# A lattice, a small conv net and three conv layers: Wu on four column tiles, the lattice's squares on ScalarE

## The chip, the cores and the metric

The kernel runs on one core of one Trainium2 chip. The core has five engines with a queue each: TensorE (PE, the matrix unit; its weight loads are shown as PEld), VectorE (DVE), ScalarE (ACT), GpSimd (POOL) and SyncE (SP). The last two are used here for memory fills and to issue copies (DMAs), which 16 DMA engines carry out. The metric is device time in microseconds (us), lower is better; three runs of the kernel before took 17346.95 us in the median.

## What is computed

The input is 32 images of 8 channels, 256x256, in float32. Four layers, each `x + f(groupnorm(x))`:

```python
# layer 0, on x = _gn(x)
drive = grid = x[:, :8]
for _ in range(15):
    mapped = R * grid * (1.0 - grid)
    local = _conv(mapped, K_local, groups=8)            # 3x3, per channel
    grid = (1.0 - BETA) * ((1.0 - EPS) * mapped + EPS * local) + BETA * drive
cml_out = jnp.clip(grid, 0.0001, 1.0 - 0.0001)
h = jax.nn.relu(_conv(x, Wp, bp))                       # 8 -> 128 channels, 3x3
nca_out = jax.nn.sigmoid(_conv(h, Wu, bu))              # 128 -> 8, 1x1
gin = jnp.concatenate([x, cml_out, nca_out], axis=1)
g = jax.nn.sigmoid(_conv(jax.nn.relu(_conv(gin, Wg1, bg1)), Wg2, bg2))
return g * cml_out + (1.0 - g) * nca_out
# layer 1: a 3x3 conv on x and weights rounded to 8-bit integers (one scale for the whole tensor)
# layer 2: a 3x3 conv in float32;  layer 3: a 5x5 mean filter per channel
```

The scale of layer 1 needs the maximum over all 32 images, so layer 0 runs over all images first, and the layers 1 to 3 follow in a second stage.

## The kernel before

**First stage.** Two strands are woven together by hand in one instruction order. `lattice(b, ahead)` runs the 15 steps of image b. `gated()` runs the net and the gate of image b-1, and is consumed piece by piece: each piece yields an estimate of its TensorE time in us, each point of the lattice yields a gap (`BLOCK`, 7.4, after a half-step), and the loop under `tc.manual_schedule()` takes pieces until the gap is filled. Image 0's lattice has no net beside it, and the last image's net no lattice. `errands(b)`, one item after each half-step, writes the normalised image to DRAM (xn_d with a border, nr_d row by row), loads the next image and takes its statistics.

**The lattice.** Channels 0 to 5 lie as patches of 16x8 pixels over the 128 partitions, 512 columns a channel, in `states[0]` and `states[1]`, three channels each. The kernel keeps v(v-1) of the state, and the constants of the map are folded into the weights. A half-step of three channels is: six matmul calls into three PSUM tiles psc (L368 with the patch, L370 with the ring of neighbours), a sum with the drive on VectorE (L378: `max` with a floor, which only catches NaNs, and an add, from PSUM to the state), the product v(v-1) in place (L384), and `spread(half)`, four copies on SyncE's queue that bring the neighbours of each patch to `rings[half]` (L246). TensorE needs these rings in the same half of the next step. `ps_c`, the pool of psc, has three buffers, and the statistics' small matmuls (L104, L111, L304) take theirs from it too.

Channels 6 and 7 are computed by VectorE alone, in blocks of four rows in `strip`: nine `tap`s a step (L317), three after half 0 and six after half 1, then a floor (L395), the product (L396), and `edges()`, two copies on SyncE's queue (L250, L251) that bring the neighbouring rows.

**The net.** For two blocks of 16 rows (one n, eight to an image) `gated` runs 16 calls ph (L606, one for each row number within the block), a relu on ScalarE into hh (L611), and the 1x1 conv Wu (L582): row r's eight outputs go to 32 PSUM partitions, tile q = r // 4, and within these to the eight that the padded weights `wu_sb[:, i, :]` pick, i = r % 4. Rows are taken four at a time, in the order 0, 4, 1, 5 and then 2, 6, 3, 7 (plus 8 in the second half), and the four Wu calls of a batch come in the next batch, in `second()`. `psum` has three buffers for ph and hh has six. The gate (L508 to L541) reads xq (nr_d), cq (cr_d), the sigmoid nh and the rows beside them, and xc, the image itself. It runs in pieces, one a batch: three conv pieces, the rest, Wg2, VectorE's blend, the store of x1, and at an image's end its statistics.

**Second stage.** Rounds over b: `layer3(b-3)`, `layer2(b-1)`, `layer1(b)`; here the framework's scheduler puts the instructions in order. `layer2` stores its result in x3_d in one copy and loads it again as y, in 16 copies, with a row of the image on each partition, as layer 3 wants it.

An fp32 matmul call is two MATMUL instructions in the profile.

Of the kernel before, what the change touches and what calls it, by code (L numbers as in the profile page):

```python
# [9 lines left out]
F32 = mybir.dt.float32  # L10
BF16 = mybir.dt.bfloat16
AF = mybir.ActivationFunctionType
ALU = mybir.AluOpType
# [34 lines left out]
RQ = 4  # L48
BLOCK = 7.4
STEPS = 15  # L50
# [16 lines left out]
def kernel(  # L67
    ctx, tc, x, patch, ring, taps, pick, wp, bp, wu, bu, wg1, wga, wgb, bg1, wg2, bg2, w1, b1, w2, b2, w3,
    w3h, eye, gavg, gavr, gsel, out,
# [22 lines left out]
    x1_d = [dram.tile([P, NPX], F32, name=f"x1_d{b}") for b in range(B)]  # L92
    x3_d = [dram.tile([P, NPX], F32, name=f"x3_d{b}") for b in range(2)]

# [73 lines left out]
    with ExitStack() as es:  # L168
# [9 lines left out]
        ring_sb = const(wt, ring, [RING, CP, P], "ring_sb")  # L178
        taps_sb = const(wt, taps, [P, 9], "taps_sb")
        pick_sb = const(wt, pick, [P, P], "pick_sb")  # L180
        wp_sb = const(wt, wp, [72, P], "wp_sb")
# [11 lines left out]


        for t in (patch_sb, ring_sb):
            flat = t.rearrange("p c m -> p (c m)")
            nc.vector.tensor_scalar(flat, flat, -R_ * (1.0 - BETA_) * EPS_, None, ALU.mult)
        nc.vector.tensor_scalar(taps_sb, taps_sb, -R_ * (1.0 - BETA_) * EPS_, None, ALU.mult)
        nc.vector.tensor_scalar(
            taps_sb[:, 4:5], taps_sb[:, 4:5], -R_ * (1.0 - BETA_) * (1.0 - EPS_), None, ALU.add  # L200
        )
        for c in range(CP):
            nc.vector.scalar_tensor_tensor(
                patch_sb[:, c, :], eye_sb, -R_ * (1.0 - BETA_) * (1.0 - EPS_), patch_sb[:, c, :],
                ALU.mult, ALU.add,
            )
# [11 lines left out]
        strip = wt.tile([P, RQ + 2, WP], F32, name="strip")  # L218
        for t in (*xbs, nh, zero, *hbs, *states, *rings, strip):
            nc.gpsimd.memset(t, 0.0)  # L220

        xn_d = [dram.tile([C, HP, WP], F32, name=f"xn_d{i}") for i in range(3)]
        nr_d = [dram.tile([P, HB, WP], F32, name=f"nr_d{i}") for i in range(3)]
        cr_d = [dram.tile([P, HB, WP], F32, name=f"cr_d{i}") for i in range(3)]
        for t in xn_d:
# [25 lines left out]
        def errands(b):  # L253
# [27 lines left out]
            if b >= 0:  # L281
                for r in four:
                    nc.gpsimd.dma_start(
                        window(
                            nr_d[b % 3], r.start * C * HB * WP,
                            [[WP, P], [C * HB * WP, 4], [1, WP]],
                        ),
                        xbs[b % 2][:, r, :],
                    )
                    yield  # L290
# [3 lines left out]
            for r in range(0, RB, 2):  # L294
                nc.vector.bn_stats(bn[:, r, :], xb[:, r, 1 : 1 + W])
                nc.vector.bn_stats(bn[:, r + 1, :], xb[:, r + 1, 1 : 1 + W])
                yield
            st, st2 = sts[(b + 1) % 2]
# [8 lines left out]
        def lattice(b, ahead):  # L307
# [42 lines left out]
            for c in range(CP):  # L350
                nc.vector.scalar_tensor_tensor(
                    inner(c), dr[:, c], 1.0, dr[:, c], ALU.subtract, ALU.mult
                )
                nc.scalar.mul(dr[:, c], dr[:, c], BETA_)
                if c == 0:
                    nc.scalar.mul(d2, d2, BETA_)
                if c % HALF == HALF - 1:
                    spread(c // HALF)
                yield 1.5
            yield 4  # L360
            for step in range(STEPS):
                for half in range(2):
# [14 lines left out]
                    for c in mine:  # L377
                        nc.vector.scalar_tensor_tensor(  # L378
                            inner(c), pss[c % HALF], FLOOR, dr[:, c], ALU.max, ALU.add
                        )  # L380
                    for c in mine:
                        v = inner(c)
                        if step < STEPS - 1:
                            nc.vector.scalar_tensor_tensor(v, v, 1.0, v, ALU.subtract, ALU.mult)  # L384
# [30 lines left out]
            for r in range(0, RB, 4):  # L415
                nc.gpsimd.dma_start(
                    window(
                        cr_d[b % 3], r * C * HB * WP,
                        [[WP, HB * CP], [C * HB * WP, 4], [1, WP]],
                    ),  # L420
                    xb[0 : HB * CP, r : r + 4, :],
                )

            row = HB * WP
            for q in range(HB // RQ):
                for c in range(2):
                    at = (C * RQ * q + CP + c) * row
                    nc.sync.dma_start(
                        window(cr_d[b % 3], at, [[WP, HB], [C * row, RQ], [1, WP]]),
                        window(  # L430
                            strip, (2 * q + c) * (RQ + 2) * WP + WP,
                            [[8 * (RQ + 2) * WP, HB], [WP, RQ], [1, WP]],
                        ),
                    )

        def beside_blocks(t, src, q, k0, n, slots):
# [3 lines left out]
            for i, (p, k) in enumerate(((P - C, k0 - 1), (0, k0 + 1))):  # L440
# [8 lines left out]
                for j, m, at in runs:  # L449
# [5 lines left out]
                    )  # L455

        place = [0]

        def gated():
# [22 lines left out]
            def gate(n, quarter):  # L482
# [95 lines left out]
            def second():  # L578
                n, pn, four = late.pop()
                for hh, r in four:  # L580
                    q, i = divmod(r, 4)
                    nc.tensor.matmul(  # L582
                        pn[32 * q : 32 * q + 32, :], wu_sb[:, i, :], hh,
                        start=i == 0, stop=i == 3,
                    )
# [8 lines left out]
            for n in range(B * NCH):  # L594
# [31 lines left out]
            second()  # L626
            yield 1.9
            while due:
# [23 lines left out]
    with ExitStack() as es:  # L652
# [80 lines left out]
        def layer2(b, x2, st):  # L733
# [60 lines left out]
        twos, threes = {}, {}  # L794
        for b in range(B + 3):
            if b >= 3:
                layer3(b - 3, *threes.pop(b - 3))
            if 1 <= b <= B:
                threes[b - 1] = layer2(b - 1, *twos.pop(b - 1))
            if b < B:  # L800
                twos[b] = layer1(b)


def laid_out(inputs):
# [33 lines left out]
    def on_rows(w):  # L838
# [42 lines left out]
    for g in range(4):  # L881
# [5 lines left out]
        ring=ring,  # L887
        taps=np.tile(K[CP:, 0].reshape(2, 9), (P // 2, 1)),
        pick=np.repeat((np.arange(P) == HB * CP)[:, None], P, 1).astype(f),
        wp=inputs["L0_conv_Wp"].transpose(2, 1, 3, 0).reshape(72, P),  # L890
# [44 lines left out]
```

## Time and profile before

| | |
|---|---|
| median of 3 runs | 17346.95 us (17322.46 to 17360.35) |
| time of the profiled execution | 17311.55 us |
| span of the profiled execution | 17309.7 us |
| TensorE clock granted, mean | 0.964 |
| shares of the chain that ended last | PE 73%, DVE 18%, DMA 5%, issue 2% |
| HBM read, written | 1078.72 MB, 404.28 MB |
| DMA moved in all | 2208.48 MB, 128 GB/s |
| first and last start of L325 (an image's lattice begins) | 34.6 us, 14016.5 us |

The span is from the first to the last instruction; 1.85 us of the execution lie around it. A line of a group gives the line of the code, engine, operation, output and inputs with their shapes, the number of instructions, then busy time in us and the mean of one in ns, then the idle time of the engine before them and who ended it. Busy time counts overlapping instructions once, so a group whose count times mean exceeds its busy time had several at work together. An engine that waits is put down to the instruction that released it.

### The profile page before, as it was taken

How to read it: one execution, taken by the hardware profiler on the slowest of the kernel's cores; microseconds unless marked ns; L12 is line 12 of the kernel's file. 1: busy time of each engine (PE TensorE's matmuls, PEld its weight loads, DVE VectorE, ACT ScalarE, POOL GpSimd, SP SyncE). 2: the span in 40 equal slices, each digit the busy share in tenths (PEclk: the TensorE clock that was granted, in tenths of full speed). 3: DMA queues.
4: the chain of work that ended last, by engine and by line, in shares of the span. 5: the costliest groups of instructions: out<-in, count | busy, mean ns of one | idle time of the engine just before them, and what ended most of it. 6: DMA issues, size and time to landing. Idle time of an engine off the chain costs nothing.

```text
span 17309.7 us, 133874 instructions
## 1 busy us (share of the span) xinstructions
PE 16500.7 (95%) x42888; PEld 6670.3 (39%) x42888; DVE 13265.9 (77%) x17529; ACT 4089.7 (24%) x5982; POOL 3931.6 (23%) x6517
## 2 busy tenths in 40 slices
PE   5999999999999999999999999999999999899999
PEld 2333333333333333333333333333333333344444
DVE  8788888888888788878888887888888884555554
ACT  0222222222222222222222222222222223111110
POOL 1222222222222222222222222222222223111111
PEclk7999999999999999999999999999999999999999
DMA  3666666666666666666666666666666665455454
GB/s 82 129 129 133 133 131 134 127 132 132 133 132 131 124 133 134 128 128 128 127 134 130 129 132 129 133 133 132 133 130 131 133 127 117 113 129 125 122 131 102
DMA packets 817532, 2208.48 MB, mean 128 GB/s; under 512 B 281741, under 2 KB 485749, under 8 KB 732741
## 3 DMA queue, kind: packets, MB, share of 16 engines
q0 software_dynamic: 464384, 1425.54, 39.8%
q1 hardware_dynamic: 352452, 774.38, 21.6%
q8 instruction: 350, 5.73, 0.2%
q14 instruction: 346, 2.83, 0.1%
HBM read 1078.72 MB, written 404.28 MB: 86 GB/s over the span
## 4 chain that ended last, share of the span: by engine, by line
PE 73%; DVE 18%; DMA 5%; issue 2%; POOL 1%; SPq 1%; ACT 0%; DVEq 0%; POOLq 0%; ACTq 0%
PE ph L606 15%; PE psc L370 12%; PE psc L368 11%; DVE acc L317 10%; PE pg L508 10%; PE pn L582 8%; PE psv L777 6%; PE psv L698 5%; DMA rings<-state 3%; DVE state L384 2%; DVE state L378 2%; PE psv L702 2%; PE psv L781 1%; PE pq L519 1%; DMA im<-xn_d 1%
## 5 line engine op out<-in xcount | busy, mean ns | idle before, releaser
L317 DVE SCALAR_TENSOR_TENSOR acc<-strip,taps_sb,acc 128x1024 f32<-128x1024 f32 x3840 | 4931.3, 1284 | 120.2
L611 ACT ACTIVATE hh<-ph,bp_sb 128x512 f32<-128x512 f32 x4096 | 2812.2, 687 | 8403.9 <-PE ph L606 8338.9
L606 PE MATMUL ph<-im,wp_sb 72*128 72x512 f32 x8192 | 4042.1, 610 | 108.7 <-DMA im<-xn_d 86.6
L378 DVE SCALAR_TENSOR_TENSOR state<-psc,flat 128x512 f32<-128x512 f32 x2880 | 1894.8, 686 | 2072.5 <-PE psc L370 2009.5
L368 PE MATMUL psc<-state,patch_sb 128*128 128x512 f32 x5760 | 2762.9, 614 | 365.9 <-DVE u L112 284.4
L370 PE MATMUL psc<-rings,ring_sb 80*128 80x512 f32 x5760 | 2796.6, 623 | 81.5 <-DMA rings<-state 81.4
L476 POOL DMA_DIRECT2D im<-xn_d x3072 | 1730.5, 568 | 3501.1 <-PE ph L606 3117.7
L606 PEld LDWEIGHTS ph<-im,wp_sb 72*128 72x128 f32 x8192 | 1486.5, 191 | 2223.6 <-issue 2074.8
L582 PE MATMUL pn<-hh,wu_sb 128*32 128x512 f32 x8192 | 2022.0, 616 | 0.0
L368 PEld LDWEIGHTS psc<-state,patch_sb 128*128 128x128 f32 x5760 | 1073.6, 193 | 1921.4 <-issue 1142.3
L370 PEld LDWEIGHTS psc<-rings,ring_sb 80*128 80x128 f32 x5760 | 1138.5, 199 | 1588.6 <-issue 1550.9
L384 DVE SCALAR_TENSOR_TENSOR state<-state 128x512 f32<-128x512 f32 x2688 | 1689.7, 685 | 0.0
L777 PE MATMUL psv<-xr,w_sb 128*128 128x512 f32 x2560 | 1159.7, 595 | 0.5 <-DVE xr L762 0.5
L541 POOL DMA_DIRECT2D x_d<-xc x256 | 152.0, 594 | 4082.8 <-DVE xc L536 4017.9
L582 PEld LDWEIGHTS pn<-hh,wu_sb 128*32 128x32 f32 x8192 | 394.0, 111 | 1469.9 <-issue 1469.9
L508 PE MATMUL pg<-xq,wg_sb 128*128 128x512 f32 x1536 | 734.7, 615 | 13.0 <-DMA xq<-nr_d 13.0
L508 PE MATMUL pg<-cq,wg_sb 128*128 128x512 f32 x1536 | 735.0, 616 | 0.0
L508 PE MATMUL pg<-nh,wg_sb 128*128 128x512 f32 x1536 | 732.8, 614 | 0.0
L698 PE MATMUL psv<-xh,w_sb 128*128 128x512 f32 x1536 | 704.8, 595 | 8.1 <-DVE xh L734 4.1
L452 POOL DMA_DIRECT2D hb<-nh x576 | 320.4, 560 | 1710.4 <-ACT nh L560 1662.8
L777 PEld LDWEIGHTS psv<-xr,w_sb 128*128 128x128 f32 x2560 | 475.7, 189 | 565.9 <-issue 561.5
L786 DVE TENSOR_TENSOR y<-psv,y 128x512 f32<-128x512 f32 x256 | 176.6, 690 | 623.3 <-PE psv L781 623.0
(155 smaller groups left out, 12270.6 us busy)
## 6 DMA issues: line engine op xcount, KB each, us to landing
im<-xn_d POOLq DMA_DIRECT2D x3072, 193.3 KB, 7.3
rings<-state SPq DMA_DIRECT2D x1920, 159.5 KB
rings<-state SPq DMA_DIRECT2D x1920, 106.3 KB
strip<-strip SPq DMA_DIRECT2D x960, 126.0 KB
xn_d<-xb POOLq DMA_DIRECT2D x128, 516.0 KB, 10.3
nr_d<-xb POOLq DMA_DIRECT2D x128, 516.0 KB, 9.0
xq<-nr_d POOLq DMA_DIRECT2D x128, 516.0 KB, 11.6
cq<-cr_d POOLq DMA_DIRECT2D x128, 516.0 KB, 13.7
```

The costliest lines, as they stand in the source:

```text
L317: nc.vector.scalar_tensor_tensor(acc, strip[:, dy : dy + RQ, dx : dx + W], taps_sb[:, 3 * dy + dx : 3 * dy + dx + 1], d2 if dy == 1 and dx ...
L368: nc.tensor.matmul(pss[-1], patch_sb[:, c, :], inner(c), start=True, stop=False)
L370: nc.tensor.matmul(pss[c % HALF], ring_sb[:, c, :], rings[half][:, c % HALF, 0 : TX * SY].rearrange("p (x y) -> p x y", y=SY)[:, :, 0:TY], ...
L378: nc.vector.scalar_tensor_tensor(inner(c), pss[c % HALF], FLOOR, dr[:, c], ALU.max, ALU.add)
L384: nc.vector.scalar_tensor_tensor(v, v, 1.0, v, ALU.subtract, ALU.mult)
L476: nc.gpsimd.dma_start(im[24 * dy : 24 * dy + 24, k, 0:run], window(xn_d[b % 3], at, [[HP * WP, C], [1, 3], [1, run]]),)
L508: nc.tensor.matmul(o, wg1_sb[:, s, dx, :], src[:, :, dx : dx + W], start=s == dx == 0, stop=False,)
L582: nc.tensor.matmul(pn[32 * q : 32 * q + 32, :], wu_sb[:, i, :], hh, start=i == 0, stop=i == 3,)
L606: nc.tensor.matmul(ph.rearrange("p (k w) -> p k w", w=W), wp_sb, im[:, :, j * WP : j * WP + W], start=True, stop=True,)
L611: nc.scalar.activation(hh, ph, AF.Relu, bias=bp_sb)
L698: nc.tensor.matmul(o, w[:, dx, :], src[:, 2 * i : 2 * i + 2, dx : dx + W], start=dx == 0, stop=False,)
L777: nc.tensor.matmul(o, w3_sb[:, dx, :], xr[:, k, 2 * g : 2 * g + 2, dx : dx + W], start=dx == 0, stop=False,)
```

## The change

- *Wu.* Rows are taken in the order 0 to 3, then 4 to 7; q and i change places, so that the four calls of a batch go to the four tiles of 32 PSUM partitions. The rows of a block thereby lie on the partitions in another order (`turn`, row r at place r % 4 * 4 + r // 4), and everything that is read or written with a row a partition group follows: the weights in `on_rows`, the writes of nr_d and cr_d, and the store of x3.
- *x for the gate.* `errands` writes the raw rows of the next image to a new DRAM tensor xr_d in this order, in four copies; `gate` loads xc from it in one copy instead of two from x.
- *Squares.* VectorE's sum is written back to PSUM, and ScalarE squares it into the state: (v - 0.5)^2 = v(v-1) + 0.25. States and rings are therefore filled with 0.25, and the constant is taken out again by `lift`, a number for each channel that is added to the drive. The first squares of an image are ScalarE's too.
- *Order.* The squares, `spread(half)` and, after half 1, `edges()` are emitted 1.7 us of the net's pieces after VectorE's part. In between `held` is not empty and the gate's statistics don't advance. BLOCK is 6.5, of which 1.7 come first; a Wu group yields 1.05 instead of 1.9.
- *Second stage.* `load1`, the load of x1, is called first in its round; x3 has the image's own layout and is stored in 16 copies, and y is loaded in two.

```diff
-BLOCK = 7.4
+BLOCK = 6.5
...
+        lift = wt.tile([P, CP], F32, name="lift")
+        nc.vector.tensor_reduce(lift, kern_sb, AX.X, ALU.add)
+        nc.vector.tensor_scalar(
+            lift, lift, 0.25 * R_ * (1.0 - BETA_) * EPS_, 0.25 * R_ * (1.0 - BETA_) * (1.0 - EPS_),
+            ALU.mult, ALU.add,
+        )
+        minus = wt.tile([P, 1], F32, name="minus")
+        nc.vector.memset(minus, -0.5)
...
-        for t in (*xbs, nh, zero, *hbs, *states, *rings, strip):
+        for t in (*xbs, nh, zero, *hbs, strip):
             nc.gpsimd.memset(t, 0.0)
+        for t in (*states, *rings):
+            nc.gpsimd.memset(t, 0.25)
...
+                if r < 8:
+                    nc.gpsimd.dma_start(
+                        window(
+                            xr_d[(b + 1) % 3], r // 2 * C * HB * W,
+                            [[W, P], [4 * C * HB * W, 4], [1, W]],
+                        ),
+                        xb[:, 2 * r : 2 * r + 4, 1 : 1 + W],
+                    )
...
-                nc.vector.scalar_tensor_tensor(
-                    inner(c), dr[:, c], 1.0, dr[:, c], ALU.subtract, ALU.mult
-                )
-                nc.scalar.mul(dr[:, c], dr[:, c], BETA_)
+                nc.scalar.activation(inner(c), dr[:, c], AF.Square, bias=minus)
+                nc.scalar.activation(
+                    dr[:, c], dr[:, c], AF.Identity, bias=lift[:, c : c + 1], scale=BETA_
+                )
...
                     for c in mine:
-                        nc.vector.scalar_tensor_tensor(
-                            inner(c), pss[c % HALF], FLOOR, dr[:, c], ALU.max, ALU.add
-                        )
-                    for c in mine:
-                        v = inner(c)
-                        if step < STEPS - 1:
-                            nc.vector.scalar_tensor_tensor(v, v, 1.0, v, ALU.subtract, ALU.mult)
-                        else:
+                        ps = pss[c % HALF]
+                        nc.vector.scalar_tensor_tensor(ps, ps, FLOOR, dr[:, c], ALU.max, ALU.add)
+                    if step == STEPS - 1:
+                        for c in mine:
                             nc.vector.tensor_scalar(
-                                dr[:, c], v, 0.0001, 1.0 - 0.0001, ALU.max, ALU.min
+                                dr[:, c], pss[c % HALF], 0.0001, 1.0 - 0.0001, ALU.max, ALU.min
                             )
-                    if step < STEPS - 1:
-                        spread(half)
...
-                        edges()
...
+                    held.append(half)
+                    yield 1.7
+                    if step < STEPS - 1:
+                        for c in mine:
+                            nc.scalar.activation(inner(c), pss[c % HALF], AF.Square, bias=minus)
+                        spread(half)
+                        if half == 1:
+                            edges()
+                    held.clear()
                     next(ahead, None)
-                    yield BLOCK
+                    yield BLOCK - 1.7
...
-                for k in range(2):
-                    nc.gpsimd.dma_start(
-                        xc[:, k, :],
-                        window(
-                            x, b * C * H * W + (k0 + k) * RB * W, [[W, RB], [H * W, C], [1, W]]
-                        ),
-                    )
+                nc.gpsimd.dma_start(xc, xr_d[b % 3][:, k0 : k0 + 2, :])
...
-                for _ in stats_parts(ps_c, bn, st, gavr_sb, "psc"):
+                parts = stats_parts(ps_c, bn, st, gavr_sb, "psc")
+                more = True
+                while more:
+                    if not held:
+                        more = next(parts, parts) is None
                     yield 0
...
-                    q, i = divmod(r, 4)
+                    i, q = divmod(r, 4)
...
-                    for rows in ((0, 4, 1, 5), (2, 6, 3, 7)):
+                    for rows in ((0, 1, 2, 3), (4, 5, 6, 7)):
...
                                 second()
-                                yield 1.9
+                                yield 1.05
...
-        def layer1(b):
+        def load1(b):
             x1 = two.tile([P, NPX], F32, name="x1")
             nc.gpsimd.dma_start(x1, x1_d[b])
+            return x1
+
+        def layer1(b, x1):
...
-            nc.gpsimd.dma_start(x3, x2)
+            for r in range(RB):
+                m = r % 4 * 4 + r // 4
+                nc.gpsimd.dma_start(
+                    window(x3, r * W, [[H * W, C], [RB * W, HB], [1, W]]),
+                    x2[C * m : C * m + C, :].rearrange("p (k w) -> p k w", w=W),
+                )
...
-            for k in range(HB):
+            for k in range(2):
                 nc.gpsimd.dma_start(
-                    y[RB * (k % 8) : RB * (k % 8) + RB, k // 8, :, :],
-                    window(x3, k * W, [[C * NPX, RB], [NPX, C], [1, W]]),
+                    y[:, k, :, :], window(x3, k * P * W, [[W, P], [H * W, C], [1, W]])
                 )
...
         for b in range(B + 3):
+            if b < B:
+                x1 = load1(b)
...
-        return a.reshape(RB * i, 3, RB * o)
+        turn = np.arange(RB) % 4 * 4 + np.arange(RB) // 4
+        return a[turn][:, :, :, turn].reshape(RB * i, 3, RB * o)
```

More of the change, by code (lines that the diff above doesn't have):

```diff
@@ L67 @@
 def kernel(
-    ctx, tc, x, patch, ring, taps, pick, wp, bp, wu, bu, wg1, wga, wgb, bg1, wg2, bg2, w1, b1, w2, b2, w3,
+    ctx, tc, x, patch, ring, taps, kern, pick, wp, bp, wu, bu, wg1, wga, wgb, bg1, wg2, bg2, w1, b1, w2, b2, w3,
     w3h, eye, gavg, gavr, gsel, out,
@@ L92 @@
     x1_d = [dram.tile([P, NPX], F32, name=f"x1_d{b}") for b in range(B)]
-    x3_d = [dram.tile([P, NPX], F32, name=f"x3_d{b}") for b in range(2)]
+    x3_d = [dram.tile([C, H, W], F32, name=f"x3_d{b}") for b in range(2)]
     def stats_parts(pool, bn, dst, avg, tag):
@@ L179 @@
         taps_sb = const(wt, taps, [P, 9], "taps_sb")
+        kern_sb = const(wt, kern, [P, CP, 9], "kern_sb")
         pick_sb = const(wt, pick, [P, P], "pick_sb")
@@ L218 @@
         strip = wt.tile([P, RQ + 2, WP], F32, name="strip")
-        for t in (*xbs, nh, zero, *hbs, *states, *rings, strip):
+        for t in (*xbs, nh, zero, *hbs, strip):
             nc.gpsimd.memset(t, 0.0)
+        for t in (*states, *rings):
+            nc.gpsimd.memset(t, 0.25)
         xn_d = [dram.tile([C, HP, WP], F32, name=f"xn_d{i}") for i in range(3)]
+        xr_d = [dram.tile([P, HB, W], F32, name=f"xr_d{i}") for i in range(3)]
         nr_d = [dram.tile([P, HB, WP], F32, name=f"nr_d{i}") for i in range(3)]
@@ L284, in errands @@
                         window(
-                            nr_d[b % 3], r.start * C * HB * WP,
-                            [[WP, P], [C * HB * WP, 4], [1, WP]],
+                            nr_d[b % 3], r.start // 4 * C * HB * WP,
+                            [[WP, P], [4 * C * HB * WP, 4], [1, WP]],
                         ),
@@ L417, in lattice @@
                     window(
-                        cr_d[b % 3], r * C * HB * WP,
-                        [[WP, HB * CP], [C * HB * WP, 4], [1, WP]],
+                        cr_d[b % 3], r // 4 * C * HB * WP,
+                        [[WP, HB * CP], [4 * C * HB * WP, 4], [1, WP]],
                     ),
@@ L426, in lattice @@
                 for c in range(2):
-                    at = (C * RQ * q + CP + c) * row
+                    at = (C * q + CP + c) * row
                     nc.sync.dma_start(
-                        window(cr_d[b % 3], at, [[WP, HB], [C * row, RQ], [1, WP]]),
+                        window(cr_d[b % 3], at, [[WP, HB], [4 * C * row, RQ], [1, WP]]),
                         window(
@@ L455, in beside_blocks @@
                     )
+        held = []
         place = [0]
@@ L626, in gated @@
             second()
-            yield 1.9
+            yield 1.05
             while due:
@@ L800 @@
             if b < B:
-                twos[b] = layer1(b)
+                twos[b] = layer1(b, x1)
 def laid_out(inputs):
@@ L888, in laid_out @@
         taps=np.tile(K[CP:, 0].reshape(2, 9), (P // 2, 1)),
+        kern=np.tile(K[:CP, 0].reshape(1, CP, 9), (P, 1, 1)),
         pick=np.repeat((np.arange(P) == HB * CP)[:, None], P, 1).astype(f),
```

## The prediction

> **What bounds the kernel now.** I read the page's busy times first, then its slices.
>
> ```profile
> PE 16500.7 (95%) x42888; PEld 6670.3 (39%) x42888; DVE 13265.9 (77%) x17529; ACT 4089.7 (24%) x5982; POOL 3931.6 (23%) x6517
> ...
> PE   5999999999999999999999999999999999899999
> ...
> DVE  8788888888888788878888887888888884555554
> ...
> PEclk7999999999999999999999999999999999999999
> ```
>
> TensorE is full in every slice but the first, where VectorE is. Is a full TensorE really the limit in each stage? Busy time by stretches answers that: inside the first image, in one steady image of layer 0, and in layers 1 to 3.
>
> ```profile
> core 0: us, PE busy (x) PEld busy (x) DVE busy (x) ACT busy (x) POOL busy (x), PEclk, DMA share, GB/s
> ...
> 200.00:300.00 100.00, 63.93 (x118) 24.94 (x116) 98.25 (x121) 0.00 (x0) 0.00 (x0) 0.80 0.33 62
> ...
> 7000.00:7450.00 450.00, 432.89 (x1131) 172.04 (x1130) 366.42 (x458) 117.99 (x173) 108.69 (x181) 0.97 0.64 130
> ...
> 16000.00:16500.00 500.00, 499.87 (x1305) 222.47 (x1304) 271.87 (x536) 60.19 (x86) 71.42 (x112) 1.00 0.53 129
> ```
>
> So image 0 is VectorE's (98 of 100 us), the next 31 lattices are TensorE's with VectorE at 81%, and everything after about 14450 us is TensorE's alone. The waits of TensorE between 450 and 14400 us show how little else it loses:
>
> ```profile
> PE psc L368 <- DVE u L112: 275.1, 60, 5.0
> PE ph L606 <- DMA im<-xn_d: 56.5, 27, 3.1
> PE psc L370 <- DMA rings<-state: 48.8, 50, 2.8
> ```
>
> These are microseconds in total, times, and the longest. Over 31 images they are 9, 2 and 1.6 us an image. An image takes 452.8 us there, from the ends of the first psc blocks of successive images (image 0 to 1: 408.8 us). Next the groups that the change touches:
>
> ```profile
> L317 DVE SCALAR_TENSOR_TENSOR acc<-strip,taps_sb,acc 128x1024 f32<-128x1024 f32 x3840 | 4931.3, 1284 | 120.2
> L611 ACT ACTIVATE hh<-ph,bp_sb 128x512 f32<-128x512 f32 x4096 | 2812.2, 687 | 8403.9 <-PE ph L606 8338.9
> ...
> L378 DVE SCALAR_TENSOR_TENSOR state<-psc,flat 128x512 f32<-128x512 f32 x2880 | 1894.8, 686 | 2072.5 <-PE psc L370 2009.5
> ...
> L582 PE MATMUL pn<-hh,wu_sb 128*32 128x512 f32 x8192 | 2022.0, 616 | 0.0
> ...
> L384 DVE SCALAR_TENSOR_TENSOR state<-state 128x512 f32<-128x512 f32 x2688 | 1689.7, 685 | 0.0
> ```
>
> L582 runs 8192 instructions of 616 ns, yet is busy only 2022 us: two run at a time. Last, the timeline of one half-step:
>
> ```profile
> 7006.57 1.91 PE L582 MATMUL pn<-hh,wu_sb 128*32 128x512 f32 x8
> 7008.41 2.84 PE L368 MATMUL psc<-state,patch_sb 128*128 128x512 f32 x6
> ...
> 7024.30 2.74 PE L370 MATMUL psc<-rings,ring_sb 80*128 80x512 f32 x6
> ...
> 7027.20 1.87 DVE L378 SCALAR_TENSOR_TENSOR state<-psc,flat 128x512 f32<-128x512 f32 x3
> ...
> 7028.99 1.89 DVE L384 SCALAR_TENSOR_TENSOR state<-state 128x512 f32<-128x512 f32 x3
> ...
> 7030.94 2.75 SPq L246 DMA_DIRECT2D rings<-state  x4
> ```
>
> Four calls of L582 (two instructions each) take 7008.41 - 7006.57 = 1.84 us. In the single records the starts come in pairs 7 ns apart, four pairs some 430 ns apart, then 523 ns to the next matmul. Three full-width calls take 2.58 us (L370, from 7024.30 to the next start at 7026.88), so 0.86 us each. Two column tiles therefore already run fully side by side.
>
> **What the Trainium skill says.** "TensorE: Matmul & The Clock Gate", Part 3, measured speedup: three column tiles gave 2.38x and four row tiles 3.07x at 512 columns. Here two tiles give 4 x 0.86 / 1.84 = 1.87x; no run shows four. "TensorEngine Tiling (Array Packing)", Key Properties: a change of tiling mode drains the array. The trace's 523 against 430 ns agrees: 0.09 us at each switch, unchanged in number. "ScalarE: Activation LUTs", table sets: cheap functions are in every set as filler (it names relu, copy, identity, abs; Square isn't in that list). The trace has Relu, Sigmoid and Identity between few loads (63 at L115, 60 at L521, 1283 ns each). The first page, Part 1, has ScalarE and VectorE as strict FIFO: a Square that waits for VectorE holds every relu behind it.
>
> **The change part by part.**
>
> 1. *Wu on four tiles.* A batch is now rows 0-3 or 4-7 on tiles 0 to 3, so its eight instructions should take two slots where four are now. Over the 1024 batches the spacing of the four slots averages 454 ns (437 in the median, about 40 batches at half clock), so two of them are worth 2 x 0.454 x 1024 = 930 us. Less two more staggered starts (2 x 7 ns) in each of two slots, 29 us: -900 us. All of it lies where TensorE is full. Bounds: nothing gained if four tiles don't overlap more than two; -930 as the other end. The yield of 1.05 for 1.9 and BLOCK 6.5 for 7.4 only keep the pacing in step with it: 32 x 0.85 = 27 us less gated work an image against 30 x 0.9 = 27 us.
>
> 2. *Squares to ScalarE.* VectorE loses L384 (1689.7 us) and L351 (118.4 us). Its load in a steady image falls from 366 to 366 - 90 x 0.686 = 305 of some 425 us. That frees nothing where TensorE is the limit. In image 0 it does: 14 steps x 6 x 0.686 = -58 us. VectorE still needs 6 x 0.63 + 9 x 1.28 + 0.70 + 1.23 = 17.2 us a step there. The ring path is shorter: 1.9 for the sums, 0.7 for the last square, 8.1 us from the issue to the last ring packet (records of the copies' packets), about 1 us for the first ring matmul, some 12 us. So VectorE stays the limit and the 58 us stand.
>
> ScalarE gets 90 squares of 0.687 us an image (as L611, also a PSUM read with a pointer bias): 118 + 62 = 180 of 425 us. Its share is no problem; its order is. The squares are emitted 1.7 us of other work after the sums. From the records, VectorE's last sum of a half 0 ends 2.1 us after TensorE's psc in the median, 3.8 at three quarters, 5.9 at nine tenths (it is still in half 1's six taps); of a half 1, 0.9 us. With 2.06 us less on VectorE and 0.9 us less period a half, I put half 0 at 0.9, 2.5 and 4.7. The last square then ends up to 5.4 us after psc in nine of ten. Behind it wait relus, and behind these TensorE, once three ph buffers are full: five calls (4.3 us) plus one pn group (1.0 us) or a pg piece (2.6 us), 5.3 to 7.9 us after psc. The psc banks, now free only after the square, are wanted again 6 us after psc. Few half-steps lose anything: I take 1 us an image (bounds 0 and 10).
>
> At the start of a lattice ScalarE has six pairs of square and Identity (1.3 us each) and the d2 scaling (1.04 us), plus relus for 9 us of TensorE (about 4 us): 13 us of work in 9, of which the ph buffers absorb about 3 and the `yield 4` the rest. The first rings leave 2 us later too. I take 2 us an image (0 to 4).
>
> The ring copies leave some 4.9 us after psc, 3.6 before for a prompt half; they land 8 to 14 us after the issue, and are wanted about 22 us after psc (24 before). That holds but for the worst: 0.5 us an image. `edges()` stays behind `spread(1)` in SyncE's queue; it waits for the clamped block 10.8 us after psc, when the rings have long been issued: nothing.
>
> 3. *Statistics.* The 9 us an image on L112 are psc waiting for a PSUM tile that VectorE reads after its taps. VectorE gets there 1.9 us sooner, TensorE 0.9: -1 us each, two an image. `held` only keeps the gate's statistics out of the stretch between sum and square. Items 2 and 3: 1 + 2 + 0.5 - 2 = +1.5, taken as 2 us x 31 = +60 us (bounds -60 and +400).
>
> 4. *Rows of x.* POOL gets 128 writes of xr_d (as nr_d at L283, 0.81 us: +103 us) and 256 instead of 512 loads of xc (0.56 us: -144 us). 67 MB more on 2208 at a DMA share of 0.64. Nothing, hidden behind six batches between a gate's loads and its use.
>
> 5. *Layers 1 to 3.* x3 is stored in 16 copies instead of one and y loaded in two instead of 16, so POOL's issues go from 17 to 18; x1 is loaded first. TensorE there is busy 499.87 of 500 us, and y has two rounds (some 160 us) to arrive: nothing. Without that cover each image would lose what the 16 issues take, 16 x 0.6 = 10 us. The permutation `turn` changes only which partition holds a row.
>
> Sum against the profiled execution (span 17309.70, time 17311.55): -900 - 58 + 60 = -898, so 16413. The median of the three runs is 17346.95, 35 us above it; on that level 16449, so 16450.
>
> **Rivals.**
>
> - *A: ScalarE's order costs more.* If each half 0 loses 0.7 us (its late tail waits longer, or rings land late), that is 15 x 31 x 0.7 = 325 us: 16775. For: the 5.9 us tail above, and the DMA share rising from 0.64. Against: 6 us of slack and VectorE lighter. Chance 0.12.
> - *B: four tiles overlap only partly.* If the two passes of a call, or the operand streams, leave three slots instead of two, half the 900 goes: 16900. For: only two tiles are seen side by side, and the page's 2.38x is for three. Against: two overlap with no loss. Chance 0.09.
> - *C: slower.* The loop closes through ScalarE's queue: Square waits for VectorE, relus wait for Square, TensorE for relus, and psc for its bank, so the lag comes back each half-step. The place is psc of every half-step, 30 x 31 of them, and it decides from 898 / 930 = 0.97 us each; at 2 us it is +1860, so 18310. Against: VectorE's idle time grows, so a lag is caught up within a half. Chance 0.05.
>
> **How the numbers follow.** The forecast has 0.74, with 16340 to 16560 as its own range (the bounds of items 2 and 3, cut to the likely). The range of 16330 to 16780 takes in A and leaves out B and C with 0.14, and some tails. A measurement here tells about 0.2% from no change: faster by more 0.94, within 0.01, slower 0.05.
>
> **What would show it.** pn's busy time near 1100 us, with four starts together; VectorE near 11460 and ScalarE near 5900 us; a steady image near 427 us and image 0 near 350; layers 1 to 3 still near 2660 us. B would show as three slots a batch; A and C as TensorE's waits on ScalarE (ph on hh, psc on a square) or on rings. I am wrong if these exceed some 4 us an image, or layers 1 to 3 show idle TensorE.

## The result: slower, and the profile after

The changed kernel takes 17976.51 us in the median of 4 runs (17938.9 to 18014.93) against 17352.36 us: ratio 1.0363, 95% interval 1.0335 to 1.0392. It is slower by 624 us where 898 less were forecast. The profiled execution (18014.93 us, span 18013.1) shows first, in the busy times and slices of its page, where to look:

```profile
PE 16230.1 (90%) x42888; PEld 6626.1 (37%) x42888; DVE 11668.1 (65%) x14652; ACT 5750.9 (32%) x8862; POOL 3954.2 (22%) x6421
...
PE   5999999999999999999999999999999977777777
...
DVE  6777777777777777777777777777777544444443
...
PEclk7999999999999999999999999999999988888888
```

TensorE has fallen from 95% to 90%. Its last eight slices, layers 1 to 3, were 8 and 9 and are 7, at a lower clock. Busy time by stretches says the same (columns as before: length, PE, PEld, DVE, ACT, POOL, clock, DMA share, GB/s):

```profile
200.00:300.00 100.00, 63.53 (x117) 24.73 (x115) 90.86 (x102) 19.73 (x30) 0.00 (x0) 0.75 0.35 65
...
7000.00:7450.00 450.00, 428.11 (x1139) 172.27 (x1138) 318.23 (x371) 169.48 (x263) 108.62 (x181) 0.93 0.66 136
...
16000.00:16500.00 500.00, 380.12 (x926) 164.30 (x924) 208.27 (x397) 44.88 (x61) 71.02 (x93) 0.86 0.42 85
```

The last row had 499.87 busy us at full clock, and now 380.12 at 0.86. The last pn matmul divides the stages: it starts at 14445.8 us (14724.6 before). So the first stage is 279 us shorter and the second, 3567 us for 2585, 982 longer. The difference, 703 us, is that of the two profiled executions; the medians lie 624 apart. A round of the second stage takes about 109 us; it took 77.

In the first stage the groups of the change behave as forecast, pn above all (count x mean is 4.5 times its busy time, so four tiles run together):

```profile
L420 ACT ACTIVATE state<-psc,minus 128x512 f32<-128x512 f32 x2688 | 1696.3, 689 | 2606.8 <-DVE psc L402 2474.2
L607 PE MATMUL pn<-hh,wu_sb 128*32 128x512 f32 x8192 | 1166.4, 640 | 0.0
```

Yet a steady image takes 445.6 us, not 427. TensorE's waits between 450 and 14400 us (us in total, times, longest):

```profile
PE psc L391 <- DVE u L112: 158.1, 60, 3.9
PE ph L631 <- DMA im<-xn_d: 116.0, 28, 6.5
PE pg L528 <- DMA xq<-nr_d: 88.6, 29, 4.7
PE ph L631 <- ACT hh L636: 80.7, 61, 2.3
PE psc L391 <- DVE stat L105: 72.5, 30, 2.5
```

Counts near 30 or 60 say that these are fixed places of each image. Their sum, some 17 us an image, doesn't explain the gap of 19 to the forecast alone, for before had waits too. The granted clock explains the rest. This is the timeline at the start of a lattice, start and duration ahead of each line:

```profile
7056.25 6.11 POOL L441 DMA_DIRECT2D cr_d<-xb  x4 [8.83 <-DVE xb L433]
7062.35 0.58 POOL L502 DMA_DIRECT2D im<-xn_d  x1
...
7071.20 2.22 POOL L502 DMA_DIRECT2D im<-xn_d  x4
...
7076.08 3.06 PE L631 MATMUL ph<-im,wp_sb 72*128 72x512 f32 x4 [3.84 <-DMA im<-xn_d]
7079.08 1.93 PE L607 MATMUL pn<-hh,wu_sb 128*32 128x512 f32 x8
```

POOL stands 8.83 us behind VectorE with the cr_d stores, the im loads are queued behind them, and TensorE waits 3.84 us. After this the pn batch takes 1.93 us; at 7056.02, 23 us earlier, the same eight instructions took 1.06. Two stretches on either side show why:

```profile
7050.00:7075.00 25.00, 22.24 (x101) 11.46 (x99) 14.50 (x16) 13.07 (x21) 14.35 (x19) 1.00 0.64 150
7077.00:7101.00 24.00, 24.00 (x41) 7.88 (x40) 0.00 (x0) 12.72 (x19) 4.09 (x8) 0.51 0.61 95
```

TensorE is busy throughout the second, at half clock, and gets through 41 instructions. So a steady image can be split, from the matmul records and the clock's records, into TensorE's idle time, half of the time at half clock (lost), and the remaining work at full clock. The means of images 2 to 31 (idle time within a slow spell counts in both, so that work comes out up to 2 us low):

| kernel | image, us | idle | at half clock | work |
|---|---|---|---|---|
| before | 452.8 | 16.7 | 29.8 | 421 |
| after | 445.6 | 23.3 | 55.2 | 395 |
| a4, two tiles | 445.1 | 13.3 | 19.2 | 422 |
| b1, squares only | 442.5 | 10.7 | 19.6 | 422 |
| b3, tiles only | 466.8 | 28.4 | 89.1 | 394 |
| b4, old second stage | 446.0 | 24.6 | 54.8 | 394 |
| c1, b1 with late cr_d | 441.9 | 10.3 | 19.1 | 422 |
| c2, b4 with late cr_d | 437.1 | 23.1 | 37.4 | 395 |

The change took 26 us of work out of each image and put back 6.6 us of idle time and 25.4 / 2 = 12.7 us of slow clock.

For the second stage, these are its groups in the changed kernel:

```profile
L723 PE MATMUL psv<-qh,w_bf 128*128 128x512 bf16 x768 | 298.8, 540 | 152.2 <-ACT qh L703 151.4
L727 PE MATMUL psv<-qb,w_bf 72*128 72x512 bf16 x256 | 122.9, 577 | 497.4 <-DMA qb<-qh 497.4
```

and the same two of the kernel before:

```profile
L698 PE MATMUL psv<-qh,w_bf 128*128 128x512 bf16 x768 | 216.5, 384 | 9.3 <-ACT qh L678 9.3
L702 PE MATMUL psv<-qb,w_bf 72*128 72x512 bf16 x256 | 97.8, 385 | 7.8 <-DMA qb<-qh 7.8
```

Layer 1 waits 497.4 us for the copies of its rows' neighbours and 152.2 us for the quantised rows themselves; before, 17 us. One round of the changed kernel in the timeline, from the load of x1 on:

```profile
15948.80 0.59 POOL L734 DMA_DIRECT2D x<-x_d  x1
...
16047.50 1.53 DVE L740 TENSOR_SCALAR tq<-x,stat 128x1024 f32<-128x1024 f32 x2
...
16052.19 5.89 PE L723 MATMUL psv<-qh,w_bf 128*128 128x512 bf16 x15 [4.80 <-ACT qh L703]
...
16058.00 3.20 SPq L143 DMA_DIRECT2D qb<-qh  x2
...
16076.02 2.31 PE L727 MATMUL psv<-qb,w_bf 72*128 72x512 bf16 x5 [17.95 <-DMA qb<-qh]
```

and of the kernel before:

```profile
16127.21 1.52 DVE L712 TENSOR_SCALAR tq<-x,stat 128x1024 f32<-128x1024 f32 x2
16129.05 2.74 PE L698 MATMUL psv<-xh,w_sb 128*128 128x512 f32 x6
...
16135.92 0.81 PE L698 MATMUL psv<-qh,w_bf 128*128 128x512 bf16 x3
...
16154.79 1.43 SPq L143 DMA_DIRECT2D qb<-qh  x2
```

Before, VectorE quantises layer 1's image while TensorE is in layer 2 (xh), and the qb copies leave under other matmuls; the qh matmuls at 16135.92 are still those of the image before. In the changed kernel the scheduler has put the quantisation behind layer 2's end; TensorE arrives at qb and waits some 18 us for the copy, every round. The load of x1 isn't late there: it lands 18 us after its issue in the median, and 78 us (median of 32 images) before VectorE begins with it. No matmul of these layers was edited: only copies, and the order of the rows.

### The profile page after: what moved, and what is told of

The parts are those of the page before. It is cut to its first block, busy times and chain, and to the rows that moved or that the text cites. A ratio compares the mean times of both kernels' runs of the same rounds, so it can differ in the third digit from the quotient of the medians.

```text
span 18013.1 us, 136438 instructions
## 1 busy us (share of the span) xinstructions
PE 16230.1 (90%) x42888; PEld 6626.1 (37%) x42888; DVE 11668.1 (65%) x14652; ACT 5750.9 (32%) x8862; POOL 3954.2 (22%) x6421
## 5 line engine op out<-in xcount | busy, mean ns | idle before, releaser
L631 PE MATMUL ph<-im,wp_sb 72*128 72x512 f32 x8192 | 4247.6, 635 | 238.3 <-DMA im<-xn_d 141.8
L402 DVE SCALAR_TENSOR_TENSOR psc<-psc,flat 128x512 f32<-128x512 f32 x2880 | 1937.4, 696 | 3713.1 <-PE psc L393 3701.4
L636 ACT ACTIVATE hh<-ph,bp_sb 128x512 f32<-128x512 f32 x4096 | 2758.8, 690 | 4778.8 <-PE ph L631 4724.1
L391 PE MATMUL psc<-state,patch_sb 128*128 128x512 f32 x5760 | 2783.4, 617 | 328.1 <-DVE u L112 166.0
L420 ACT ACTIVATE state<-psc,minus 128x512 f32<-128x512 f32 x2688 | 1696.3, 689 | 2606.8 <-DVE psc L402 2474.2
L631 PEld LDWEIGHTS ph<-im,wp_sb 72*128 72x128 f32 x8192 | 1534.4, 198 | 2478.4 <-issue 1925.9
L391 PEld LDWEIGHTS psc<-state,patch_sb 128*128 128x128 f32 x5760 | 1082.5, 194 | 1916.7 <-issue 1238.2
L809 PE MATMUL psv<-xr,w_sb 128*128 128x512 f32 x2560 | 1162.0, 596 | 14.9 <-DVE xr L794 14.9
L607 PE MATMUL pn<-hh,wu_sb 128*32 128x512 f32 x8192 | 1166.4, 640 | 0.0
L528 PE MATMUL pg<-xq,wg_sb 128*128 128x512 f32 x1536 | 880.0, 719 | 88.6 <-DMA xq<-nr_d 88.6
L776 POOL DMA_DIRECT2D x_d<-x x512 | 366.3, 728 | 2624.3 <-DVE x L771 2427.2
L809 PEld LDWEIGHTS psv<-xr,w_sb 128*128 128x128 f32 x2560 | 480.5, 190 | 598.8 <-issue 591.5
## 6 DMA issues: line engine op xcount, KB each, us to landing
nr_d<-xb POOLq DMA_DIRECT2D x128, 516.0 KB, 10.2
```

Of the source, the lines that this page charges most:

```text
L391: nc.tensor.matmul(pss[-1], patch_sb[:, c, :], inner(c), start=True, stop=False)
L402: nc.vector.scalar_tensor_tensor(ps, ps, FLOOR, dr[:, c], ALU.max, ALU.add)
L420: nc.scalar.activation(inner(c), pss[c % HALF], AF.Square, bias=minus)
L528: nc.tensor.matmul(o, wg1_sb[:, s, dx, :], src[:, :, dx : dx + W], start=s == dx == 0, stop=False,)
L607: nc.tensor.matmul(pn[32 * q : 32 * q + 32, :], wu_sb[:, i, :], hh, start=i == 0, stop=i == 3,)
L631: nc.tensor.matmul(ph.rearrange("p (k w) -> p k w", w=W), wp_sb, im[:, :, j * WP : j * WP + W], start=True, stop=True,)
```

## The experiments

The expectations name their theories by letters and say what each means: P puts the second stage's loss on x3's pieces and L on the place of x1's load; for the first stage, T has four tiles gain nothing net, H has the loss in stalls and the slow clock that follows them, K, its rival, in the stalls alone, and Q in the squares on ScalarE. Single times below stand beside one run of the kernel before on the same chip (17348.04 us for the runs a, 17319.55 for b).

**a1: the load of x1 back into layer 1.**

```diff
-            if b < B:
-                x1 = load1(b)
...
-                twos[b] = layer1(b, x1)
+                twos[b] = layer1(b)
```

> The changed kernel with the load of x1 back inside layer1. Theory P (the sixteen copies that store x3, with their cost in the scheduler's eyes, have changed the order of the second stage, so that layer 1's chain stands open before TensorE): a round of the second stage stays at 100 to 115 us instead of 77, total 17800 to 18150 us. Theory L (the load of x1 put first did it): rounds of about 77 us, total about 17000 us.

17732.61 us, between the two forecasts and much nearer to P's. The second stage is 3318 us: the load's place cost some 250 us on top of the pieces, and 730 us stay.

**a2: the kernel before, with x3 in pieces and nothing else.**

```diff
-            nc.gpsimd.dma_start(x3, x2)
+            for r in range(RB):
+                nc.gpsimd.dma_start(
+                    window(x3, r * W, [[H * W, C], [RB * W, HB], [1, W]]),
+                    x2[C * r : C * r + C, :].rearrange("p (k w) -> p k w", w=W),
+                )
...
-            for k in range(HB):
+            for k in range(2):
```

> The kernel before with one edit: x3 in the image's layout, stored in sixteen copies and loaded in two. Theory P: rounds of 100 to 115 us, total 18100 to 18500 us. Theory L: rounds stay at 77 us, total 17300 to 17400 us.

17976.82 us, somewhat less than P's range: first stage as before (14744), second 3231, so 646 us from this edit alone. In one stretch of it TensorE has lost both time and clock:

```profile
16000.00:16500.00 500.00, 417.06 (x1056) 183.47 (x1055) 221.63 (x438) 45.65 (x67) 69.59 (x109) 0.91 0.36 91
```

The waits are not those of the changed kernel's timeline:

```profile
15890.28 0.59 POOL L747 DMA_DIRECT2D x_d<-x  x1 [72.99 <-DVE x L743]
...
15909.35 0.58 POOL L709 DMA_DIRECT2D x<-x_d  x1
...
15922.11 1.53 DVE L712 TENSOR_SCALAR tq<-x,stat 128x1024 f32<-128x1024 f32 x2 [16.06 <-DMA x<-x_d]
...
15926.72 5.12 PE L698 MATMUL psv<-qh,w_bf 128*128 128x512 bf16 x15 [31.56 <-ACT qh L678]
```

Here the load of x1 (L709) stands in POOL's queue behind stores of x3 (L747), which wait for layer 2's end, and VectorE waits for it: 185 us in all in this stage, 220 in a1, 3 in the kernel before. So without load1 the load is late; with it, in the changed kernel, the load is early and VectorE's order is late.

**a3: the changed kernel, x3 in four stores and y in 16 loads.**

```diff
-            for r in range(RB):
-                m = r % 4 * 4 + r // 4
+            for q in range(4):
...
-            for k in range(2):
+            for k in range(HB):
```

> The changed kernel with x3 as before (one row of pieces a partition), stored in four copies and loaded in sixteen; x1's load stays first. Theory P: rounds back near 77 us and TensorE full there, total 16950 to 17150 us. Theory L: rounds stay near 109 us, total 17900 to 18100 us.

17499.96 us; the second stage is 3038 us with rounds of some 92. A miss for both theories: fewer stores recover half, not all.

**a4: the changed kernel with two tiles in a batch.**

```diff
-                    for rows in ((0, 1, 2, 3), (4, 5, 6, 7)):
+                    for rows in ((0, 1, 4, 5), (2, 3, 6, 7)):
```

> The changed kernel with rows in the order 0, 1, 4, 5 and 2, 3, 6, 7, so that a batch of Wu uses two column tiles instead of four; nothing else. The second stage stays as it is. Theory H (four tiles do what they should, and stalls of TensorE with the half clock that follows them take most of it back): pn's busy time returns to about 2000 us and the first stage grows by 300 to 850 us, since longer blocks leave fewer stalls; total 18300 to 18850 us. Theory T (four tiles at once are what lowers the clock, so nothing is gained by them): clock of a steady image back to 0.97, first stage within 100 us of the changed kernel's, total 17900 to 18100 us.

18003.33 us, so T's number holds and H's doesn't. The first stage ends at 14463 us, 17 later than with four tiles. All that the four tiles save had been given back: the table has for a4 27 us more work, 10 less idle and 36 less slow clock, of which half, 18, is lost time.

**b1: the kernel before with the squares on ScalarE.** Their later place in the order and `held` come with them; nothing else does.

```diff
+                        nc.vector.scalar_tensor_tensor(ps, ps, FLOOR, dr[:, c], ALU.max, ALU.add)
...
+                            nc.scalar.activation(inner(c), pss[c % HALF], AF.Square, bias=minus)
```

> The kernel before with the squares on ScalarE and nothing else of the change: two column tiles, x and x3 as before, BLOCK 7.4. Theory P: the second stage is the one before (rounds of 77 us, 2585 us in all), since the copies of x3 are untouched. For the first stage, if the squares alone are the gain that the changed kernel shows there, it ends at 14430 to 14500 us and the total is 17020 to 17090 us; if they add stalls of their own, the first stage stays at 14700 or more and the total is 17290 us or more.

16973.22 us, 346 less than before and 50 less than forecast. The wait that stands first in the list above was 275.1 us in the kernel before; here:

```profile
PE psc L379 <- DVE u L112: 136.9, 60, 3.1
```

Whether the lighter VectorE or `held`, which keeps the gate's statistics out of the stretch between sum and square, took it down was not tried apart.

**b2: the changed kernel, cr_d stored from SyncE's queue.**

```diff
-                nc.gpsimd.dma_start(
+                nc.sync.dma_start(
```

> The changed kernel with the four stores of cr_d at the end of a lattice on SyncE's queue instead of GpSimd's, so that the loads of im behind them don't wait for VectorE. Theory H (a stall of TensorE costs its own length and then half of the slow clock that follows it): the wait for im at the start of a lattice, 4.7 us an image, and most of the 22 us of half clock after it go, 8 to 16 us an image, 250 to 500 us in all: total 17470 to 17730 us. Theory K (the slow clock there comes from the transposes and short matmuls of the lattice's end, not from the stall): at most the stall itself goes, and the 22 us stay: total 17830 to 18000 us.

17882.24 us. Slow clock at the lattice's start falls from 22 to 8 us an image, but the rings, on the same queue, are late by 3.9 us there: the wait had moved. The total lies in K's range, though the 22 us that K has stay are gone: this run doesn't decide between H and K.

**b3: the changed kernel with the squares back on VectorE (and a3's stores).**

```diff
-                            nc.scalar.activation(inner(c), pss[c % HALF], AF.Square, bias=minus)
+                            nc.vector.scalar_tensor_tensor(v, v, 1.0, v, ALU.subtract, ALU.mult)
```

> Four column tiles with the squares left on VectorE (the kernel of the four stores with the squares of the kernel before). The second stage is that of the four stores, about 3038 us. Theory Q (the squares in ScalarE's queue bring the stalls): the four tiles show their full worth, the first stage ends at 13850 to 14000 us, total 16890 to 17040 us. Theory H (any shorter block leaves stalls at the same places, POOL's queue and the statistics, and each is followed by half clock): first stage 14300 to 14700 us, total 17340 to 17740 us.

18192.53 us, a miss for Q and for H, whose range ended at 17740. The first stage ends at 15143.9 us, 419 later than before, with the same 394 us of work as the changed kernel. The waits have VectorE's names:

```profile
PE psc L389 <- DVE u L112: 194.5, 59, 3.3
PE psc L389 <- DVE stat L105: 134.3, 29, 5.2
...
PE psc L389 <- DVE state L399: 99.0, 59, 2.1
PE ps L104 <- DVE state L399: 76.4, 25, 3.9
```

Here a shorter TensorE step without a shorter VectorE step was a loss: 28.4 us idle and 89.1 at half clock in each image.

**b4: the changed kernel with the second stage of before, word for word.** x1 is stored in four pieces a gate, in the image's order, in place of x3's.

```diff
-            for r in range(RB):
-                m = r % 4 * 4 + r // 4
...
+            nc.gpsimd.dma_start(x3, x2)
...
-            for k in range(2):
+            for k in range(HB):
```

> The changed kernel with the second stage of the kernel before, word for word; the rows are put back into their order when x1 is stored, in four copies a gate instead of one. Theory P: second stage 2585 us with TensorE full; the first stage as in the changed kernel, 14400 to 14550 us; total 16990 to 17140 us. If something else of the change slows the second stage (the state that the first leaves behind), it stays above 3000 us, total above 17450 us.

17049.37 us; the second stage is 2585 us, as before:

```profile
16000.00:16500.00 500.00, 499.84 (x1321) 222.37 (x1320) 286.25 (x568) 66.60 (x95) 70.00 (x112) 1.00 0.50 124
```

P stands in the main: all 982 us are in what this run puts back, x3's copies, the place of the x1 load and the order of the rows in these layers. The first two account for 646 (a2) and some 250 (a1); the 87 that are left were not tried apart.

**c1, c2, c3: the im loads freed.** In c1 (b1) and c2 (b4) the stores of cr_d are issued one gap into the next lattice, so that no im load is behind them; c3 is c2 with the gate's loads a batch earlier and the first scaling on VectorE.

```diff
+        def settle():
+            while owed:
+                b = owed.pop()
+                for r in range(0, RB, 4):
...
+            settle()
...
-            for r in range(0, RB, 4):
...
+            owed.append(b)
...
-                due.setdefault(batch + 6, []).append(gate(n, quarter))
+                due.setdefault(batch + 5, []).append(gate(n, quarter))
```

> The kernel before with the squares on ScalarE, and the cr_d stores of a lattice issued only after the next lattice's first im loads on POOL (nothing else). Its image has at the lattice's start a TensorE wait for im of 3.4 us and 8.6 us at half clock. H (a stall costs itself and half of the slow-clock time that follows it): both go, 31 x (3.4 + 4.3) = 240 us, so 16740 us (16680 to 16830), and the half-clock time of a steady image falls from 19.6 to about 11 us. K (the slow clock has another cause, a stall costs only itself): 31 x 3.4 = 105 us at most, 16870 to 16970, half-clock time as before. If the im wait merely gives way to another wait there, 16970.

16905.62 us, ratio 0.9763 (0.9748 to 0.9777), and the first stage ends 42 us earlier than b1's. Some 28 of these 42 us lie between image 0 and image 1, at one long wait for im. A miss for H's number: the im wait goes, and another takes its place, so idle and slow clock stay as in b1. Both of K's forecasts hold, but as the idle time didn't fall, the run doesn't test H against K.

```profile
PE psc L396 <- DMA rings<-state: 49.0, 26, 3.2
```

> Four column tiles, the squares on ScalarE, the rows of the changed kernel, the second stage of the kernel before, and the cr_d stores issued after the next lattice's first im loads. The changed kernel's im wait is 4.7 us of each image and the half-clock time beside it 22.3 us. H: 31 x (4.7 + 11.1) = 490 us less than the 17049 us of the same kernel without the deferral: 16560 us (16480 to 16700), half-clock time of a steady image from 55 to about 33 us. K: 31 x 4.7 = 146 us less, 16900, half-clock time unchanged. T (four tiles are worth nothing beside two, because a fuller TensorE is throttled anyway): not below c1's time, about 16740 or more.

16766.95 us, ratio 0.9684 (0.9665 to 0.9702), the fastest of all. Against b4's 17049.37 it is 282 us less. In the half-step at the lattice's start TensorE's idle time fell only from 5.3 (b4) to 3.9 us an image, but from image 3 on it is in pieces of at most 2.6 us, where b4 had one of 2.7 to 4.6 us in each, and the half-clock time there fell from 21.5 to 2.9 us: 31 x (1.4 + 18.6 / 2) = 332 us, less what grew at later places. K (no change in slow clock) falls. T's strict form falls too: c2 is 139 us below c1, though its number (16740 or more) held. H's own number, 16560, is missed, as the clock is still low behind the other waits:

```profile
PE psc L406 <- DVE u L112: 158.1, 60, 3.9
PE ph L645 <- ACT hh L650: 124.4, 121, 2.3
PE pg L538 <- DMA xq<-nr_d: 107.8, 34, 6.4
```

> As the run with four tiles and deferred stores, and each gate's loads (xq, rings) begun one batch earlier, and the scaling at the lattice's start on VectorE in place of ScalarE's Identity. In the changed kernel xq's wait is some 3.0 us and the rings' wait 2.9 us of each image. H: 31 x (5.9 + about as much half-clock loss) = 370 us less than its neighbour: 16200 us (16050 to 16400). K: 31 x 5.9 = 183 us less, 16700. If the waits are for something else than the time of issue (the queue, VectorE's rows), no change against the neighbour.

16983.7 us, ratio 0.9805 (0.9789 to 0.9821): slower than c2, where H and K both had it faster. xq's wait went; im's came back, longer than in any other run shown between 450 and 14400 us:

```profile
PE ph L646 <- DMA im<-xn_d: 272.2, 49, 11.8
```

## Why the prediction was wrong

*What bounds the kernel.* Right, as far as it went: TensorE in the second stage was at 499.87 of 500 us. The view shows that TensorE's inputs came in time, not with how much to spare.

*Item 1, four tiles, -900.* The mechanism was right. L607's busy time is 1166.4 us (forecast near 1100), and c2's work is 26.7 us an image below c1's, 31 x 26.7 = 828 us. B is refuted. But the working took time off TensorE as if whatever feeds it kept up. What remained of it was 17 us beside a4, and 139 us (c2 beside c1) once one stall was broken up.

*Items 2 and 3, +60 and -58.* The +60 was wrong in sign, the -58 in size. The squares on ScalarE, with their order and `held`, gave 346 us (b1). The working had the L112 wait fall by 2 us an image; it lost 275.1 - 136.9 = 138 us in all, over twice that, and the slow clock fell from 29.8 to 19.6 us an image. Image 0, where 58 us were expected, gave 22.7 (image 0 to 1: 386.1 us for 408.8); VectorE is busy there for 90.86 of 100 us, no longer 98, so it isn't the only limit any more. A, waits on ScalarE's order, did occur at L631 (80.7 us in total), below its 325.

*The slow clock.* This is the term missing from each sum: stalls were counted at their own length. In the changed kernel an image has 6.6 us more idle time and loses 12.7 more to the slow clock, 31 x 19.3 = 598 us, against 31 x (421.2 - 394.7) = 822 of work saved. That leaves 224; with image 0's 23 and some 26 of work in the last image's net, 273 of the measured 279.

*Item 4, rows of x.* Its "nothing" was not tried alone. TensorE's waits for xq, which is loaded from the same queue (POOL's), went from 13.0 to 88.6 us in all, but a4 has the same copies of x and only 6.8, so they came with the four tiles. a4's first stage ends 76 us later than b1's; the rows of x and the pacing (BLOCK and the yields) are what it has beside b1 there.

*Item 5, layers 1 to 3, "nothing".* **This is the step that failed**, and it turned a gain of 279 into a loss: 982 us. It asked when y arrives and what POOL's 16 issues cost, and its price without cover, 10 us an image, was for these issues. The loss was 31 us an image. Idle TensorE in these layers, which the prediction named as the sign of its error, was there, but in the changed kernel not at y: L809, which reads y's rows, waits 14.9 us in all. a2 shows that 16 stores and two loads in place of one and 16 make 646 us in the kernel before, and a1 that the load's place adds some 250; b4 bounds all that is left.

What the step missed is layer 1: when x1 is there, and when VectorE quantises it. The order of every queue in this stage, POOL's too, is made by a scheduler. In a2 it has the load of x1 behind stores that wait for layer 2's end. In the changed kernel the load is early, but layer 1's quantisation sits behind layer 2 instead of within it, and qb's copy is exposed. "Load first" and "pieces" were weighed as copies, not as inputs to an order. How the scheduler comes to that order was not measured, nor how much of the loss in a3, where TensorE waits most for the copies of layer 3 (L813), is copies that land late.

*Rival C* had the right side for the wrong reason: ScalarE's queue doesn't close a loop; the waits of psc (L391) on a square sum to 15.6 us in 30 times, where 0.97 us in each half-step were needed.

## What to carry to other kernels

Price a stall of TensorE by what follows it: itself plus half of the slow-clock time, which can be more (12 us behind a wait of 3.84 here). Before taking work off a full engine, ask for every feeder whether it keeps up with the shorter period, and lighten those first (b1 gained without touching TensorE's work). Where a scheduler sets the order, an edit to a copy can change every queue's order: look at what a load now stands behind, and at when each engine takes up its work, before weighing the copies themselves.

## What was not expected of the hardware

The slow spells come in multiples of 3413 ns (3.4, 6.8, 10.2 and 23.9 us were seen), which agrees with the window that the Trainium skill, "TensorE: Matmul & The Clock Gate", Part 1, states. The same part has the clock fall after an idle window of about 3.4 us; of the changed kernel's 193 spells between 450 and 14400 us, only 19 have TensorE idle for the whole 3413 ns ahead of them, by the matmul records. But in each of the 193 it is idle for at least 1.1 us of these 3413 ns, 2.2 in the median (as 1.36 us ahead of L104 at 5598 us). The measurement decides: below 3.4 us a gap isn't safe. It also bears on theory T: no spell began in dense work alone. And 3.84 us of waiting was followed by 23.9 us at half clock with TensorE busy throughout: why it stays slow that long, and whether four tiles have a part in that, is open.

The timeline has four column tiles run a batch of four Wu calls in 7057.01 - 7056.02 = 0.99 us, where a full-width call takes 0.86: 4 x 0.86 / 0.99 = 3.5 times, against 1.87 with two tiles.
